# Layer 0, step one: four engines in source order, in-place tiles in one deep ring, normalizing in place, Toeplitz rows on the storing queue

## The chip, the cores and the metric

The kernel runs on one core of a Trainium2 chip. The core has five engines with a queue each: TensorE (PE, with its weight loads shown apart as PEld), VectorE (DVE), ScalarE (ACT), GpSimd (POOL) and SyncE (SP, which here only issues transfers). Transfers (DMAs) are issued by SP, ACT or POOL and carried out by 16 DMA engines. The metric is the time of one execution on the device in microseconds (us); lower is better.

## What is computed

Four layers, each adding a block's output to x (8 images of 56 x 56 positions and 192 channels, float32). The change concerns the first part of layer 0 alone:

```python
def _gn(v, G=32, eps=1e-5):              # group norm over 6 channels x all positions
    g = v.reshape(B_, H_, W_, G, C_ // G)
    ...
    return ((g - m) / jnp.sqrt(s + eps)).reshape(v.shape)

# layer 0, D1 = 576
    p = jax.nn.silu(x @ p_w.T + p_b)
    q = jax.nn.silu(x @ q_w.T + q_b)
    v = jax.nn.silu(x @ v_w.T + v_b)
    ...
    a1 = _rpe_mlp(rpe_input, t1_w0, ...) * decay      # 111 coefficients a channel
    a2 = _rpe_mlp(rpe_input, t2_w0, ...) * decay
    qv = q * v
    o1 = _toeplitz(qv.reshape(b * h, w, D1), a1).reshape(b, h, w, D1)   # along a row
    o2 = _toeplitz(jnp.transpose(qv, (0, 2, 1, 3)).reshape(b * w, h, D1), a2)   # along a column
    ...
    out = p * (o1 + o2)
    return out @ o_w.T + o_b
```

## The kernel before

**Two steps through DRAM.** Layer 0 runs as two steps. Step one computes qv for all eight images and writes it to two DRAM arrays, `left` (rows as they are) and `right` (transposed in the image), in blocks of 64 channels ("subs", nine of them). Behind the qv rows each array holds 64 Toeplitz rows a sub, made from the coefficients. Step two (`layer0_mix`) loads blocks of both (`layer0_block`, tiles `lt` and `rt` of 1.8 MB each), multiplies them on TensorE, gates with p and projects. The change is in step one; later stages are as they were.

**Step one.** Per image b: `layer0_load` (L353) fetches x, a tile of 128 x 3 x 1568 (two halves of the image times 64 channels, three channel blocks), from POOL's queue. `layer0_in` (L358) takes twelve pieces of statistics (L157), two tiny matmuls over the groups (L176) with a square root on ACT between (L186), and writes the normalized image to another tile `xn` (L371, DVE). `layer0_qv` (L374) then runs over 14 pairs of image rows (`PH`) and two halves n of the 576 outputs. One such (i, n) is called a group below; there are 8 x 14 x 2 = 224. A group is 12 matmuls (q and v, three channel blocks, both image halves s), recorded as 24 because each float32 matmul is two records; then, for each s, the bias out of PSUM (L393, DVE), SiLU in place (L394, ACT) and q*v (L395, DVE) into the tile `qv`. After the second n, three stores for each s go out from SP's queue: one to `left` (L398) and two to `right` (L403). The `qv` ring has 3 tiles, `act` 4, and PSUM holds 4 tiles of two banks under the tag "qv", shared with every small matmul of this step.

**What is put between.** `between[i]` lists small jobs that are traced after row pair i: the coefficient network (`toeplitz_rows`, L227, 13 pieces with PSUM tiles of their own), Toeplitz rows and zero rows (L295 and L300, 128 DRAM to DRAM transfers issued by ACT), the attention mask of layer 1 (`build_bias_mask`), its weights (`layer1_weights`), and `layer0_in` of the next image after row pair 4.

**What sets the order.** In step one no order is written out: the build's scheduler ranks the traced instructions by its own estimate of times and lays down each engine's queue. Each engine then works through its queue strictly in that order and waits where an operand isn't there. Later stages have stretches under `tc.manual_schedule`, in which the named engines keep the order of the source.

Of the kernel before, what the change touches and what calls it, by code (L numbers as in the profile page):

```python
# [10 lines left out]
F32 = mybir.dt.float32  # L11
AF = mybir.ActivationFunctionType
ALU = mybir.AluOpType
# [4 lines left out]
B, H, W, C = 8, 56, 56, 192  # L18
NT = H * W
HC = 96  # L20
TT = 392
NTT = NT // TT
D1 = 576
DCH = [(0, 128), (128, 128), (256, 128), (384, 128), (512, 64)]
NSUB = D1 // 64
# [37 lines left out]
NH = NT // 2  # L63
NTH = NH // TT
PH = NPAIR // 2
# [24 lines left out]
def kernel(ctx: ExitStack, tc: tile.TileContext, a: dict, out: bass.AP):  # L90
    nc = tc.nc
# [21 lines left out]
    gmath = resident("gmath")  # L113
# [7 lines left out]
    eps5 = const.tile([128, 1], F32, name="eps5")  # L121
# [14 lines left out]
    none = dram.tile([QR], F32, name="none")  # L136
# [17 lines left out]
    def gn_piece(st, x, t):  # L154

        for j in range(3):
            nc.vector.bn_stats(st[:, j, t], x[:, j, bass.ts(t, TT)])  # L157

    def gn_aggregate(st, mv):
        nc.vector.bn_aggr(mv, st.rearrange("p j t s -> p (j t s)"))  # L160

    def gn_finish(mv, sc, sh, pool, psum, ptag):


        n = mv.shape[1]

        def over_groups(v, name):
            if ptag == "mm":
                ps = psum.tile([128, 512], F32, name=name, tag="mm", bufs=3)
            elif ptag == "y":  # L170
                ps = psum.tile([128, TT], F32, name=name, tag="y")
            elif ptag == "gn":
                ps = psum.tile([128, 3], F32, name=name, tag="gn", bufs=1)
            else:
                ps = psum.tile([128, 2, 512], F32, name=name, tag=ptag)[:, 0]
            nc.tensor.matmul(ps[:, 0:n], gmath, v, start=True, stop=True)  # L176
            return ps[:, 0:n]

        mean = pool.tile([128, n], F32, name="gh_mean")
        nc.vector.tensor_copy(mean, over_groups(mv[:, :, 0], "gh_m"))  # L180
        d = pool.tile([128, n], F32, name="gh_d")
        nc.vector.tensor_tensor(d, mv[:, :, 0], mean, ALU.subtract)
        nc.vector.tensor_tensor(d, d, d, ALU.mult)
        nc.vector.tensor_tensor(d, d, mv[:, :, 1], ALU.add)
        yield
        nc.scalar.activation(sc, over_groups(d, "gh_v"), AF.Sqrt, bias=eps5)  # L186
        nc.vector.reciprocal(sc, sc)
        nc.vector.scalar_tensor_tensor(sh, mean, -1.0, sc, ALU.mult, ALU.mult)

    def run(steps):  # L190
        for _ in steps:
            pass
# [34 lines left out]
    def toeplitz_rows(psum, pool, rows):  # L227
# [16 lines left out]
        k = 1  # L244
        while k < 55:
            n = min(k, 55 - k)
# [9 lines left out]
        for i in range(2):  # L256
            m = f"m{i + 1}_"
            h = pool.tile([32, 111], F32, name=f"h{i}")
# [3 lines left out]
        for l in range(3):  # L262
            yield
            for i in range(2):
                ps = psum.tile([128, 2, 512], F32, name="hps", tag="qv")
# [6 lines left out]
        for c, (d0, M) in enumerate(DCH):  # L272
            yield
            cos = []
            for i in range(2):
                ps = psum.tile([128, 2, 512], F32, name="aps", tag="qv")
# [7 lines left out]
            for i in range(2):  # L284
                ps = psum.tile([128, 2, 512], F32, name="cps0", tag="qv")
# [7 lines left out]
        parts = [z[toep_row(0):].rearrange("(s k) n -> k s n", k=64) for z in (left, right)]  # L293

        def row(i, w0):  # L295
            nc.scalar.dma_start(
                parts[i][w0], coef[i][:, 55 - w0:111 - w0].rearrange("s l d -> s (l d)")
            )

        def zeros(i, k):  # L300
            nc.scalar.dma_start(parts[i][k], none.partition_broadcast(NSUB))

        rows += [lambda i=i, k=k: zeros(i, k) for i in range(2) for k in range(W, 64)]
        rows += [lambda i=i, w0=w0: row(i, w0) for i in range(2) for w0 in range(W)]
# [48 lines left out]
    def layer0_load(b, pool):  # L353
        x = pool.tile([128, 3, NH], F32, name="x0")
        nc.gpsimd.dma_start(x, a["x"][b])
        return x

    def layer0_in(b, x, pool, psum):  # L358

        sc, sh = scsh[:, 0, b:b + 1], scsh[:, 1, b:b + 1]  # L360
        st = pool.tile([128, 3, NTH, 6], F32, name="gh_st")
        for t in range(NTH):
            gn_piece(st, x, t)
        mv = pool.tile([128, 1, 2], F32, name="gh_mv")
        gn_aggregate(st, mv[:, 0])
        run(gn_finish(mv, sc, sh, pool, psum, "qv"))
        xn = pool.tile([128, 3, NH], F32, name="xn0")
        n = NH if b else TT
        for t in range(NH // n):
            ts = bass.ts(t, n)  # L370
            nc.vector.tensor_scalar(xn[:, :, ts], x[:, :, ts], sc, sh, ALU.mult, ALU.add)  # L371
        return xn

    def layer0_qv(b, xn, pool, psum, w_qv, b_qv, between):  # L374

        lv, rv = (
            z[qv_row(b, 0):qv_row(b, 0) + NSUB * W].rearrange("(s h) (w d) -> s h w d", h=W, d=64) for z in (left, right)
        )
        for i in range(PH):
            qv = pool.tile([2 * W, 2, D1], F32, name="qv", bufs=3)  # L380
            for n in range(2):
                ns = slice(n * D1 // 2, (n + 1) * D1 // 2)
                ps = [psum.tile([2 * W, 2, 512], F32, name=f"qv{s}", tag="qv") for s in range(2)]
                for which in range(2):
                    for j in range(3):
                        for s in range(2):
                            nc.tensor.matmul(  # L387
                                ps[s][:, which, 0:D1 // 2], xn[64 * s:64 * s + 64, j, bass.ts(i, 2 * W)],
                                w_qv[64 * s:64 * s + 64, j, which, ns], start=(j == 0), stop=(j == 2),
                            )  # L390
                for s in range(2):
                    act = pool.tile([2 * W, 2, D1 // 2], F32, name="act", bufs=4)
                    nc.vector.tensor_tensor(act, ps[s][:, :, 0:D1 // 2], b_qv[:, :, ns], ALU.add)  # L393
                    nc.scalar.activation(act, act, AF.Silu)  # L394
                    nc.vector.tensor_tensor(qv[:, s, ns], act[:, 0], act[:, 1], ALU.mult)  # L395
            for s in range(2):
                h0 = H // 2 * s + 2 * i
                nc.sync.dma_start(  # L398
                    lv[:, h0:h0 + 2].rearrange("s h w d -> (h w) s d"),
                    qv[:, s].rearrange("t (s d) -> t s d", d=64),  # L400
                )
                for r in range(2):
                    nc.sync.dma_start(  # L403
                        rv[:, :, h0 + r].rearrange("s w d -> w s d"),
                        qv[r * W:(r + 1) * W, s].rearrange("w (s d) -> w s d", d=64),
                    )
            for step in between[i]:
                step()

    def layer0_block(b, s, raws):  # L410

# [910 lines left out]
    with ExitStack() as st:  # L1322
        pool = st.enter_context(tc.tile_pool(reuse_waits="tile", name="qv", bufs=2))
        psum = st.enter_context(tc.tile_pool(reuse_waits="tile", name="qvp", bufs=4, space=PSUM))
        w_qv = resident("w_qv", nc.scalar, pool)
        b_qv = pool.tile([2 * W, 2, D1], F32, name="b_qv", bufs=1)
        nc.scalar.dma_start(b_qv.rearrange("p a d -> p (a d)"), a["b_qv"].partition_broadcast(2 * W))
        tz = st.enter_context(tc.tile_pool(reuse_waits="tile", name="tz", bufs=2))
        x = layer0_load(0, pool)
        xn = layer0_in(0, x, pool, psum)  # L1330
        rows, masks = [], []
        coefs, bias = toeplitz_rows(psum, tz, rows), build_bias_mask(psum, tz, masks)
        centred = layer1_weights(tz, psum)

        def pop(todo, n=1):
            for _ in range(min(n, len(todo))):
                todo.pop(0)()

        for b in range(nimg):

            between = {i: [lambda i=i: pop(rows, 2 if i % 3 == 1 else 1)] for i in range(PH)}
            if b == 0:
                for i in range(PH):
                    between[i].insert(0, lambda: [next(coefs, None) for _ in range(2)])
                between[10].append(lambda: next(bias, None))
            elif b == 1:
                between[6].append(lambda: next(bias, None))
                between[12].append(lambda: pop(masks))
            elif b == 2:
                for i in range(6):  # L1350
                    between[2 * i].append(lambda: next(centred, None))
            if b:
                between[9].append(lambda: pop(masks))
            ahead = []
            if b + 1 < nimg:
                x = layer0_load(b + 1, pool)
                between[4].append(lambda: ahead.append(layer0_in(b + 1, x, pool, psum)))
            layer0_qv(b, xn, pool, psum, w_qv, b_qv, between)
            xn = ahead[0] if ahead else None
        pop(rows, len(rows))  # L1360
        pop(masks, len(masks))
    with ExitStack() as st:
# [8 lines left out]
        images, x = ExitStack(), []  # L1371
# [312 lines left out]
```

## Time and profile before

| | us |
|---|---|
| median of three runs | 5757.5 |
| lowest, highest | 5750.73, 5760.37 |
| the profiled run | 5770.6 |
| its span | 5768.8 |
| PE, DVE, ACT, POOL busy in the span | 5181.2, 3336.5, 2169.1, 1420.2 |
| first and last matmul record of step one (L387) | 28.6 and 846.7 |
| last store of step one issued until | 857.7 |

The profile is one execution. A group of instructions is given as line, engine, operation, names, shapes, count, busy time, mean duration in ns, and the idle time of the engine before it with what ended that. PEclk or "granted clock" is the share of TensorE's full clock that it was allowed. A line "A <- B" among the waits says that A stood for B. The DMA share is the mean busy share of the 16 engines. The granted clock over the whole span is 0.957.

### The profile page before, as it was taken

What the parts mean: (1) busy time and instruction counts of PE and PEld (TensorE: products, weight loads), DVE (VectorE), ACT (ScalarE), POOL (GpSimd) and SP (SyncE); (2) the same over time, 40 slices, a digit from 0 to 9 for tenths busy, and PEclk for the clock granted to TensorE, in tenths of its full rate; (3) what the DMA queues carried; (4) which work ended last, traced back from release to release, by engine and by line L of the source; (5) the groups of instructions that cost most, each with busy time, mean ns of one, the idle gap of its engine ahead of it and who ended that gap; (6) DMA issues with size and microseconds to landing.
All of it is one profiled execution on the core that took longest, in us unless ns stands there. A gap on an engine that the chain in (4) does not pass through costs nothing. (4 is left out here: it accounts for less than half of the span.)

```text
span 5768.8 us, 116138 instructions
## 1 busy us (share of the span) xinstructions
PE 5181.2 (90%) x50342; PEld 3376.1 (59%) x50342; DVE 3336.5 (58%) x4710; ACT 2169.1 (38%) x2908; POOL 1420.2 (25%) x1107
## 2 busy tenths in 40 slices
PE   6898998999899979999997989999788798999999
PEld 4568765666666645555554657676344597444444
DVE  5777774555555546566665868888778202433331
ACT  2333443333333423333332004555476400433333
POOL 2100004444444424433342013333101101100100
PEclk8999999999999989999998989999899899999999
DMA  6888986776677633222222866666687598212211
GB/s 179 204 211 216 206 182 258 264 264 258 247 262 264 222 92 82 69 75 76 69 65 76 260 235 218 227 232 209 160 232 215 222 328 295 78 62 77 76 41 26
DMA packets 721922, 1013.94 MB, mean 176 GB/s; under 512 B 486376, under 2 KB 645444, under 8 KB 694644
## 3 DMA queue, kind: packets, MB, share of 16 engines
q1 hardware_dynamic: 706352, 940.12, 52.4%
q0 software_dynamic: 8512, 40.62, 2.1%
q10 hardware_dynamic: 6548, 25.78, 1.4%
q8 instruction: 396, 6.49, 0.5%
q14 instruction: 114, 0.93, 0.0%
HBM read 676.92 MB, written 345.97 MB: 177 GB/s over the span
## 5 line engine op out<-in xcount | busy, mean ns | idle before, releaser
L387 PE MATMUL qv<-w_qv_sb,xn 64*112 64x288 f32 x5376 | 711.3, 421 | 48.6 <-DVE act L393 45.4
L425 POOL COPY lc<-lt 128x896 f32<-128x896 f32 (+1 forms) x320 | 552.5, 1751 | 640.9 <-PE op L433 543.1
L387 PEld LDWEIGHTS qv<-w_qv_sb,xn 64*112 64x112 f32 x5376 | 558.5, 182 | 195.5 <-DVE act L393 58.1
L394 ACT ACTIVATE act<-act 112x576 f32<-112x576 f32 x448 | 300.6, 683 | 466.8 <-DVE act L393 427.4
L433 PE MATMUL op<-rc,lc 128*56 128x56 f32 x9216 | 339.1, 221 | 102.1 <-POOL lc L425 64.9
L433 PEld LDWEIGHTS op<-rc,lc 128*56 128x56 f32 x9216 | 307.8, 135 | 177.9 <-POOL lc L425 103.5
L1289 PE MATMUL ph<-y,w_sb 64*128 64x392 f32 x2304 | 397.7, 497 | 6.5 <-ACT hid L1293 6.5
L1300 PE MATMUL po<-hid,w_sb 128*64 128x392 f32 x2304 | 386.3, 494 | 0.0
L393 DVE TENSOR_TENSOR act<-qv,b_qv 112x576 f32<-112x576 f32 x448 | 320.7, 752 | 92.7 <-PE qv L387 92.4
L1307 DVE TENSOR_TENSOR x<-x,z 128x392 f32<-128x392 f32 x96 | 67.0, 698 | 524.2 <-ACT z L1305 524.2
L425 ACT COPY rc<-rt 128x896 f32<-128x896 f32 (+1 forms) x160 | 256.3, 1606 | 249.7 <-PE op L433 227.2
L805 PE MATMUL qk_ps<-xr,wg 64*96 64x392 f32 x1536 | 334.2, 538 | 1.8 <-DVE xr L752 1.7
L1016 PE MATMUL cv<-zc,wt 128*128 128x224 f32 x1536 | 313.6, 356 | 24.2 <-DMA zc<-pd 24.2
L1016 PEld LDWEIGHTS cv<-zc,wt 128*128 128x128 f32 x1536 | 291.0, 190 | 67.5 <-issue 51.2
L1289 PEld LDWEIGHTS ph<-y,w_sb 64*128 64x128 f32 x2304 | 220.0, 188 | 175.9 <-issue 25.5
L445 PE MATMUL pj<-xn,w_p_sb 64*128 64x392 f32 x1536 | 309.8, 511 | 12.4 <-DVE xn L533 8.2
L1190 PE MATMUL cps<-zc,wt 128*128 128x224 f32 x1536 | 300.2, 356 | 18.2 <-DMA zc<-zd 16.8
L1190 PEld LDWEIGHTS cps<-zc,wt 128*128 128x128 f32 x1536 | 289.6, 189 | 28.7 <-issue 21.3
L466 PE MATMUL y<-pp,w_o_sb 128*64 128x392 f32 x1536 | 285.9, 501 | 4.8 <-DVE x L474 4.1
L459 DVE TENSOR_TENSOR pp<-pp,ot 128x784 f32<-128x784 f32 x128 | 124.2, 970 | 284.8 <-ACT pp L450 272.9
L1300 PEld LDWEIGHTS po<-hid,w_sb 128*64 128x64 f32 x2304 | 162.7, 137 | 213.8 <-issue 213.8
L1031 POOL TENSOR_TENSOR rows<-rows,loc 128x896 f32<-128x896 f32 x96 | 220.8, 2300 | 261.7 <-ACT rows L1027 201.9
(233 smaller groups left out, 8895.1 us busy)
## 6 DMA issues: line engine op xcount, KB each, us to landing
lt<-left SPq DMA_DIRECT2D x72, 1792.0 KB
rt<-right SPq DMA_DIRECT2D x72, 1792.0 KB
left<-qv SPq DMA_DIRECT2D x224, 252.0 KB
right<-qv SPq DMA_DIRECT2D x448, 126.0 KB
wt<-in_band_dram SPq DMA_DIRECT2D x23, 2048.0 KB
wt<-in_band_dram SPq DMA_DIRECT2D x11, 4096.0 KB
zc<-pd SPq DMA_DIRECT2D x187, 232.0 KB
pd<-pt SPq DMA_DIRECT2D x7, 5568.0 KB
```

The source lines that it names most:

```text
L387: nc.tensor.matmul(ps[s][:, which, 0:D1 // 2], xn[64 * s:64 * s + 64, j, bass.ts(i, 2 * W)], w_qv[64 * s:64 * s + 64, j, which, ns], start ...
L393: nc.vector.tensor_tensor(act, ps[s][:, :, 0:D1 // 2], b_qv[:, :, ns], ALU.add)
L394: nc.scalar.activation(act, act, AF.Silu)
L425: copy(c[:, 0:nu], raw.rearrange("p (w u d) -> p u d w", u=nu, d=64 // nu)[:, :, d0:d0 + 8])
L433: nc.tensor.matmul(op[64 * u:64 * u + W, i, :], lc[:, u, i], rc[:, u, i], start=True, stop=True)
L445: nc.tensor.matmul(ps[0:M, s, 0:TT], w_p[64 * s:64 * s + 64, j, d0:d0 + M], xn[64 * s:64 * s + 64, j, ts], start=(j == 0), stop=(j == 2),)
L466: nc.tensor.matmul(y[64 * s:64 * s + 64], w_o[0:M, c, 64 * j:64 * j + 64], pp[0:M, s], start=(c == gated[0][0]), stop=(c == gated[-1][0]),)
L805: nc.tensor.matmul(in_pairs(ps[s]), wg[64 * s:64 * s + 64, j, c0:c0 + HC], in_slots(xr[64 * s:64 * s + 64], (3 * g + j) * GW), start=(j == ...
L1016: nc.tensor.matmul(dst, wt[:, c4 + i, 128 * q:128 * q + 128], zc[:, :, c4 + i, q:q + NPAIR], start=(q == 0), stop=(q == 1),)
L1190: nc.tensor.matmul(dst.rearrange("p (b n) -> p b n", n=NPAIR), wt[:, c4 + i, q * OP:(q + 1) * OP], zc[:, :, c4 + i, q:q + NPAIR], start=(q ...
L1289: nc.tensor.matmul(ps[:, s, 0:TT], w0[64 * s:64 * s + 64, j, m * 128:(m + 1) * 128], y[64 * s:64 * s + 64, j, ts], start=(j == 0), stop=(j ...
L1300: nc.tensor.matmul(ps[64 * s:64 * s + 64], w1[:, m, 64 * j:64 * j + 64], hid[:, m, s], start=(m == 0), stop=(m == 5),)
```

## The change

Five things change in step one.

1. PE, ACT, DVE and POOL keep the order of the source (`manual_schedule`); SP's queue is still laid down by the scheduler. `layer0_in` becomes a generator that is advanced by one piece after each group from the eighth on.
2. A group's outputs are 5 subs or 4 subs (320 or 256 columns) in turn, not 288 each. Bias, SiLU and the product all work in one tile `act`, of which there are 14; there is no `qv` tile. A group's product is traced one group later, for s = 0 on DVE and for s = 1 on POOL, followed by its stores: three per s and group, where there were three per s and pair of groups.
3. x is normalized in place in four pieces, on DVE for the first image and on POOL for the others. So a tile of x is in use until its image's last matmul, and the load of the image after next waits for that.
4. Toeplitz and zero rows are issued by SP, three of them in every four groups, and cannot begin before the coefficients are done.
5. `between` counts groups, not row pairs. The first coefficient piece and the 42 small loads of the mask's table (`raw`) are traced ahead of the first image.

```diff
@@ -293,12 +293,12 @@
...
         def row(i, w0):
-            nc.scalar.dma_start(
+            nc.sync.dma_start(
                 parts[i][w0], coef[i][:, 55 - w0:111 - w0].rearrange("s l d -> s (l d)")
             )
 
         def zeros(i, k):
-            nc.scalar.dma_start(parts[i][k], none.partition_broadcast(NSUB))
+            nc.sync.dma_start(parts[i][k], none.partition_broadcast(NSUB))
@@ -360,52 +360,77 @@
         sc, sh = scsh[:, 0, b:b + 1], scsh[:, 1, b:b + 1]
         st = pool.tile([128, 3, NTH, 6], F32, name="gh_st")
         for t in range(NTH):
-            gn_piece(st, x, t)
-        mv = pool.tile([128, 1, 2], F32, name="gh_mv")
-        gn_aggregate(st, mv[:, 0])
-        run(gn_finish(mv, sc, sh, pool, psum, "qv"))
-        xn = pool.tile([128, 3, NH], F32, name="xn0")
-        n = NH if b else TT
-        for t in range(NH // n):
-            ts = bass.ts(t, n)
-            nc.vector.tensor_scalar(xn[:, :, ts], x[:, :, ts], sc, sh, ALU.mult, ALU.add)
-        return xn
-
-    def layer0_qv(b, xn, pool, psum, w_qv, b_qv, between):
+            for j in range(3):
+                nc.vector.bn_stats(st[:, j, t], x[:, j, bass.ts(t, TT)])
+                yield
+        mv = pool.tile([128, 2], F32, name="gh_mv")
+        gn_aggregate(st, mv)
+        yield
+        yield
+        of = [psum.tile([128, 2, 512], F32, name=n, tag="qv")[:, 0, 0:1] for n in ("gh_m", )]
+        nc.tensor.matmul(of[0], gmath, mv[:, 0:1], start=True, stop=True)
+        mean, d = (pool.tile([128, 1], F32, name=n) for n in ("gh_mean", "gh_d"))
+        nc.vector.tensor_copy(mean, of[0])
+        nc.vector.tensor_tensor(d, mv[:, 0:1], mean, ALU.subtract)
+        nc.vector.tensor_tensor(d, d, d, ALU.mult)
+        nc.vector.tensor_tensor(d, d, mv[:, 1:2], ALU.add)
+        yield
+        yield
+        of.append(psum.tile([128, 2, 512], F32, name="gh_v", tag="qv")[:, 0, 0:1])
+        nc.tensor.matmul(of[1], gmath, d, start=True, stop=True)
+        nc.scalar.activation(sc, of[1], AF.Sqrt, bias=eps5)
+        yield
+        nc.vector.reciprocal(sc, sc)
+        nc.vector.scalar_tensor_tensor(sh, mean, -1.0, sc, ALU.mult, ALU.mult)
+        for t in range(NTH):
+            xs = x[:, :, bass.ts(t, TT)]
+            (nc.gpsimd if b else nc.vector).tensor_scalar(xs, xs, sc, sh, ALU.mult, ALU.add)
+            if t < 2:
+                yield
+
+    def layer0_qv(b, x, pool, psum, w_qv, b_qv, between):
 
         lv, rv = (
             z[qv_row(b, 0):qv_row(b, 0) + NSUB * W].rearrange("(s h) (w d) -> s h w d", h=W, d=64) for z in (left, right)
         )
+        later = []
+
+        def multiply(i, s0, s1, acts):
+            n = 64 * (s1 - s0)
+            for s in range(2):
+                eng = (nc.vector, nc.gpsimd)[s]
+                eng.tensor_tensor(acts[s][:, 0, 0:n], acts[s][:, 0, 0:n], acts[s][:, 1, 0:n], ALU.mult)
+            for s in range(2):
+                h0 = H // 2 * s + 2 * i
+                qv = acts[s][:, 0, 0:n].rearrange("t (s d) -> t s d", d=64)
+                nc.sync.dma_start(lv[s0:s1, h0:h0 + 2].rearrange("s h w d -> (h w) s d"), qv)
+                for r in range(2):
+                    nc.sync.dma_start(rv[s0:s1, :, h0 + r].rearrange("s w d -> w s d"), qv[r * W:(r + 1) * W])
+
         for i in range(PH):
-            qv = pool.tile([2 * W, 2, D1], F32, name="qv", bufs=3)
-            for n in range(2):
-                ns = slice(n * D1 // 2, (n + 1) * D1 // 2)
+            for at, (s0, s1) in enumerate(((0, 5), (5, NSUB))):
+                n = 64 * (s1 - s0)
                 ps = [psum.tile([2 * W, 2, 512], F32, name=f"qv{s}", tag="qv") for s in range(2)]
                 for which in range(2):
                     for j in range(3):
                         for s in range(2):
                             nc.tensor.matmul(
-                                ps[s][:, which, 0:D1 // 2], xn[64 * s:64 * s + 64, j, bass.ts(i, 2 * W)],
-                                w_qv[64 * s:64 * s + 64, j, which, ns], start=(j == 0), stop=(j == 2),
+                                ps[s][:, which, 0:n], x[64 * s:64 * s + 64, j, bass.ts(i, 2 * W)],
+                                w_qv[64 * s:64 * s + 64, j, which, 64 * s0:64 * s1], start=(j == 0), stop=(j == 2),
                             )
+                acts = [pool.tile([2 * W, 2, 320], F32, name="act", bufs=14) for _ in range(2)]
                 for s in range(2):
-                    act = pool.tile([2 * W, 2, D1 // 2], F32, name="act", bufs=4)
-                    nc.vector.tensor_tensor(act, ps[s][:, :, 0:D1 // 2], b_qv[:, :, ns], ALU.add)
-                    nc.scalar.activation(act, act, AF.Silu)
-                    nc.vector.tensor_tensor(qv[:, s, ns], act[:, 0], act[:, 1], ALU.mult)
-            for s in range(2):
-                h0 = H // 2 * s + 2 * i
-                nc.sync.dma_start(
-                    lv[:, h0:h0 + 2].rearrange("s h w d -> (h w) s d"),
-                    qv[:, s].rearrange("t (s d) -> t s d", d=64),
-                )
-                for r in range(2):
-                    nc.sync.dma_start(
-                        rv[:, :, h0 + r].rearrange("s w d -> w s d"),
-                        qv[r * W:(r + 1) * W, s].rearrange("w (s d) -> w s d", d=64),
+                    nc.vector.tensor_tensor(
+                        acts[s][:, :, 0:n], ps[s][:, :, 0:n], b_qv[:, :, 64 * s0:64 * s1], ALU.add
                     )
-            for step in between[i]:
-                step()
+                for s in range(2):
+                    nc.scalar.activation(acts[s][:, :, 0:n], acts[s][:, :, 0:n], AF.Silu)
+                for step in later:
+                    step()
+                later = [lambda now=(i, s0, s1, acts): multiply(*now)]
+                for step in between[2 * i + at]:
+                    step()
+        later[0]()
@@ -1327,10 +1352,15 @@
         nc.scalar.dma_start(b_qv.rearrange("p a d -> p (a d)"), a["b_qv"].partition_broadcast(2 * W))
         tz = st.enter_context(tc.tile_pool(reuse_waits="tile", name="tz", bufs=2))
         x = layer0_load(0, pool)
-        xn = layer0_in(0, x, pool, psum)
         rows, masks = [], []
         coefs, bias = toeplitz_rows(psum, tz, rows), build_bias_mask(psum, tz, masks)
         centred = layer1_weights(tz, psum)
+        st.enter_context(tc.manual_schedule(
+            engines={mybir.EngineType.PE, mybir.EngineType.Activation, mybir.EngineType.DVE, mybir.EngineType.Pool}
+        ))
+        next(coefs)
+        next(bias)
+        run(layer0_in(0, x, pool, psum))
 
         def pop(todo, n=1):
             for _ in range(min(n, len(todo))):
@@ -1338,25 +1368,27 @@
 
         for b in range(nimg):
 
-            between = {i: [lambda i=i: pop(rows, 2 if i % 3 == 1 else 1)] for i in range(PH)}
+            between = {i: [lambda i=i: pop(rows, 1 if i % 4 else 0)] for i in range(2 * PH)}
             if b == 0:
-                for i in range(PH):
-                    between[i].insert(0, lambda: [next(coefs, None) for _ in range(2)])
-                between[10].append(lambda: next(bias, None))
+                for i in range(2 * PH):
+                    between[i].append(lambda: next(coefs, None))
             elif b == 1:
-                between[6].append(lambda: next(bias, None))
-                between[12].append(lambda: pop(masks))
+                between[13].append(lambda: next(bias, None))
+                between[25].append(lambda: pop(masks))
             elif b == 2:
                 for i in range(6):
-                    between[2 * i].append(lambda: next(centred, None))
+                    between[4 * i + 1].append(lambda: next(centred, None))
             if b:
-                between[9].append(lambda: pop(masks))
-            ahead = []
+                between[19].append(lambda: pop(masks))
+            ahead = iter(())
             if b + 1 < nimg:
-                x = layer0_load(b + 1, pool)
-                between[4].append(lambda: ahead.append(layer0_in(b + 1, x, pool, psum)))
-            layer0_qv(b, xn, pool, psum, w_qv, b_qv, between)
-            xn = ahead[0] if ahead else None
+                following = layer0_load(b + 1, pool)
+                ahead = layer0_in(b + 1, following, pool, psum)
+                for i in range(7, 2 * PH):
+                    between[i].append(lambda: next(ahead, None))
+            layer0_qv(b, x, pool, psum, w_qv, b_qv, between)
+            run(ahead)
+            x = following
         pop(rows, len(rows))
         pop(masks, len(masks))
     with ExitStack() as st:
```

In the instruction order as built, SP has 800 DMAs more (672 stores, 128 rows), ACT 128 fewer, POOL 252 instructions more and DVE 231 fewer. No block of step two is issued before the last store of step one. From the second block of step two on, each engine has nearly the order that it had.

## The prediction

> **What bounds the stage now.** The change touches only layer 0's first step, the program's first 858 us. The chain that ended last does not help: its pieces begin at 4033 us. So I read stretches, then waits, then the timeline. The page's groups first:
>
> ```profile
> L387 PE MATMUL qv<-w_qv_sb,xn 64*112 64x288 f32 x5376 | 711.3, 421 | 48.6 <-DVE act L393 45.4
> ...
> L394 ACT ACTIVATE act<-act 112x576 f32<-112x576 f32 x448 | 300.6, 683 | 466.8 <-DVE act L393 427.4
> ...
> L393 DVE TENSOR_TENSOR act<-qv,b_qv 112x576 f32<-112x576 f32 x448 | 320.7, 752 | 92.7 <-PE qv L387 92.4
> ```
>
> A group is 24 of the L387 matmul records (half the outputs of two row pairs); there are 5376/24 = 224. DVE needs 2 x 752 for the bias and 2 x 461 ns for q*v (L395), 2.43 us a group; ACT 2 x 683 = 1.37 us. Stretches of 25 us for L387 alone (busy and count of PE, of weight loads, granted clock, DMA share, GB/s):
>
> ```profile
> 50.00:75.00 25.00, 13.59 (x88) 9.39 (x90) 0.73 0.86 239
> ...
> 275.00:300.00 25.00, 25.00 (x210) 18.56 (x208) 1.00 0.95 214
> ...
> 325.00:350.00 25.00, 14.29 (x90) 10.13 (x88) 0.73 0.73 199
> ...
> 775.00:800.00 25.00, 25.00 (x210) 18.56 (x208) 1.00 0.88 181
> ```
>
> At its best TensorE does 210 records in 25 us: 2.86 us a group. 224 of them are 641 us, but the groups take from 28.6 to 847 us, 3.65 us each. Some 175 us are lost in holes, with the clock down to 0.73 beside them. The waits over the first 1120 us (total, times, longest), then one hole in the timeline:
>
> ```profile
> ACT act L394 <- DVE act L393: 427.4, 230, 12.3
> ...
> DVE gh_st L157 <- DMA x<-in_x_dram: 40.3, 6, 7.7
> ```
>
> ```profile
> 324.75 0.54 POOL L355 DMA_DIRECT2D x<-in_x_dram  x1 [53.37 <-DVE xn L371]
> ...
> 336.31 1.97 DVE L157 BATCH_NORM_STATS2 gh_st<-x 128x6 f32<-128x392 f32 x4 [6.74 <-DMA x<-in_x_dram]
> ...
> 339.03 0.68 ACT L394 ACTIVATE act<-act 112x576 f32<-112x576 f32 x1 [8.68 <-DVE act L393]
> ...
> 344.80 14.20 PE L387 MATMUL qv<-w_qv_sb,xn 64*112 64x288 f32 x94 [2.23 <-DVE act L393]
> ```
>
> The reader sees an ordering fault. The next image's load starts at 324.75, DVE's queue already has that image's statistics at its head, and DVE stands 6.74 us for the transfer; finished matmuls keep their PSUM tiles, so TensorE stops too. Image 0 loses most: between 29 and 150 us only 552 records (23 groups, 5.3 us each).
>
> The other resource is the stores. Their queue, at PE's full pace without Toeplitz rows and with them:
>
> ```profile
> 785.13 0.31 SPq L398 DMA_DIRECT2D left<-qv  x1
> 785.49 1.57 SPq L403 DMA_DIRECT2D right<-qv  x2
> ```
>
> ```profile
> 159.37 0.90 SPq L398 DMA_DIRECT2D left<-qv  x1
> 160.31 1.93 SPq L403 DMA_DIRECT2D right<-qv  x2
> ```
>
> Each group issues such a triple. It costs 1.9 to 2.4 us without rows in flight, 2.7 to 2.9 with them, and then SP hardly rests. All engines by stretches (PE, PEld, DVE, ACT, POOL, clock, DMA share, GB/s):
>
> ```profile
> 725.00:850.00 125.00, 122.07 (x1008) 90.26 (x1004) 101.08 (x172) 58.63 (x87) 2.60 (x3) 1.00 0.88 181
> 850.00:900.00 50.00, 27.23 (x506) 19.77 (x508) 18.16 (x20) 18.06 (x17) 25.32 (x16) 0.76 0.89 342
> ```
>
> **Two rules of the skill.** "DMA: Bandwidth & Descriptors", Specifications, asks for transfers of at least 512 B for line rate. The two rows above agree: with 256 B pieces (64 floats) a share of 0.88 moves 181 GB/s, with long rows 0.89 moves 342. Splitting a store by subs leaves the pieces at 256 B, so I keep the DMA work per byte. The same page, "Issuing engines are not separate DMA queues", says that all queues use the same 16 engines and another issuer saves only issue time. The trace agrees: rows on ACT's queue raise SP's triple from about 2.2 to 2.75 us. So I book the rows' DMA time as unchanged, and only their issue as moved.
>
> **Part by part.**
> *Source order, with statistics spread one per group from the eighth group on.* It removes the holes. The load of image b+1 is issued as image b starts (its tile is free when b-1's last matmul is done); 7 groups are 20 us, the load's median landing 11.5 us, so DVE should find it there. Seven image turns and image 0's preparation held the 175 us. Not all goes: each of image 0's 13 coefficient steps takes two of the four PSUM tiles and makes TensorE wait for two biases, about 0.75 + 0.75 us less a matmul of its own, 1.2 us; 16 us in all. The two statistics matmuls shift the ring by one tile, about 2 us an image; the Sqrt table loads stay (2 x 1.28 us, under ACT's slack of 1.5 us a group). At the front POOL must issue 42 `raw` loads at 617 ns (26 us) before the second image and its first product, at about 41 us. By then four groups are done; the ring of 14 tiles holds 7 groups, so this is hidden. Without that cover it would cost some 10 us.
> *Product.* One of two goes to POOL. It has no such row here; the nearest are
>
> ```profile
> L1214 POOL TENSOR_TENSOR yl<-yl,dwb 128x448 f32<-128x448 f32 x12 | 11.2, 936 | 54.8 <-DMA yl<-yd 54.8
> ...
> L1135 POOL TENSOR_SCALAR zp<-x2o,sc,sh 128x1568 f32<-128x1568 f32 x24 | 43.8, 1836 | 263.0 <-DVE sh L188 150.0 <-PE tp L1097 56.8 <-PE po L1110 26.8
> ```
>
> 2.1 ns an element (2.6 in L1031): 0.6 to 0.75 us for 288 on average, of a 2.9 us group. Normalizing is 4 x 1176 elements at 1.17 ns, 5.5 us an image, in the last four groups; the first piece serves the next four slices, so TensorE need not wait for the last. POOL thus holds 28 x 0.7 + 5.5 = 25 of 81 us. DVE falls to 2 x 0.752 + 0.461 = 1.96 us a group and loses a 2.73 us block an image. Neither is the bound; worth nothing alone.
> *Chunks of 5 and 4 subs.* The same columns and weight loads: 3.2 and 2.6 us in turn, zero on average.
> *Stores.* Twice as many, half as long: 6 per group. SP has to issue 1344 instead of 672, and 128 rows that ACT issued at 0.69 us (88 us, leaving ACT). Smallest issues in the trace are 0.31 (left) and 0.42 us (right): 2 x 0.31 + 4 x 0.42 = 2.3 us a group, the floor if it is per instruction; in proportion to descriptors it stays 2.2. Rows add 0.75 x 0.69 = 0.5 us a group while they last. Ceiling: if today's means (0.65 and 1.03 us) did not shrink at all, 5.4 us. I take 2.3 to 2.6, plus rows.
> *DMA work.* 0.88 x 2.90 = 2.55 us a group of full share. The mean share from 29 to 850 us is 0.85: 698 us. Of that 571 are stores, 7 x 6.3 = 44 images (2.35 MB at the 384 GB/s that 342/0.89 gives), 19 the four blocks of step two fetched early, which leaves 64, under 0.45 us a row.
>
> **The sum.** Start 28.6 us. Image 0: 28 x 2.95 + 16 = 99, to 128. Images 1 to 5 carry 21 rows each: 71.4 + 6.3 + 9.4 = 87 us of DMA against 80 us of TensorE; at a share of 0.97, 90 each, to 578. Image 6 (11 rows) 85, to 663. Image 7 81 and small waits 4, to 748; last stores about 753 instead of 857.7. So 105 us come off the step, now at the pace of stores, no longer of an order.
> Then something is given back. In the built order of the changed kernel no block of step two is fetched before the last store; before, two left and two right blocks were there (issues from 400.8 us on). Four blocks of 1.8 MB are 7.3/0.384 = 19 us, less the 4 us that the kernel before waited from its last issue to its next load: 15 us (5 if the first gate's wait for x, 11.4 us there, covers some; 20 if nothing does). Later stages have the same order. Net 90 to 95 us: the profiled 5770.6 (span 5768.8) becomes 5678. The median of the runs shown is 0.23% under the profiled run, so 5665.
>
> **Rivals.**
> (a) PE's pace: packets' time stretches when there is slack, so the share isn't work that must be done. For it: 210 records in 25 us with rows in flight at 0.95. Against: SP at 23 to 25 of 25 us there. 28.6 + 99 + 7 x 84 = 716, gain 141 - 15 = 126: 5632. 25%.
> (b) SP's issue at 3.4 us a group (half sizes cost a little over the floor, rows on top): 28.6 + 224 x 3.4 + 15 = 805, gain 53 - 15 = 38: 5720. 12%.
> (c) Slower: one mechanism, at SP's queue: an issue has a price that doesn't fall with size, or the eight completion semaphores that the DMAs of the hardware queues use in turn hold SP back (eight half-size stores in flight; a 14 KB transfer alone took 1.97 us until its reader's issue). It decides from (857.7 - 15 - 28.6 - 10)/224 = 3.59 us a group, 0.53 us a DMA with rows. At 0.6 us: 6 x 0.6 + 0.4 = 4.0 us, 933 us, +75 + 15: 5848. For it: right stores cost 1.03 us in the mean and SP is full; against: that follows contention (4.4 us a triple beside an image load, 2.1 alone). 11%.
> (d) Nothing gained: new in-order waits (POOL, ACT, SP) eat what the holes gave. 2%.
>
> **Numbers.** The forecast has 50%. Range 5625 to 5735: it takes in (a) and (b) and leaves out (c) and little else. Under 0.2% (11 us) a measurement can't tell from no change. Faster 0.50 + 0.25 + 0.12 less a little = 0.86; same 0.03; slower 0.11.
>
> **What would show it.** Right: no DVE wait for x over 2 us, groups under 3.3 us from image 1 on, the L387 successor's last record between 730 and 755, DMA share above 0.93 in the row phase, a hole of 10 to 20 us of little TensorE work at the turn to step two. Wrong: SP issues over 0.5 us each with PE's clock falling, or waits of multiply and bias for DMAs.

## The result, and the profile after

| | before | after |
|---|---|---|
| median of the runs beside each other (4 of each), us | 5757.2 | 5851.4 |
| ratio, 95% interval | | 1.0163, 1.0145 to 1.0180 |
| span of the profiled run, us | 5768.8 | 5843.2 |
| last matmul record of step one, us | 846.7 | 903.8 |
| last store of step one issued until, us | 857.7 | 928.7 |
| first product of step two, us | 854.4 | 941.3 |

The change makes the kernel slower by 94 us. The forecast was 5665, and its range ended at 5735. Step two starts 86.9 us later, so the loss is in step one and at the turn to step two.

The groups of the page after, against those of L387, L393 and L394 before (line, engine, operation, shapes, count, busy and mean ns, idle time before and what ended most of it):

```profile
L417 PE MATMUL qv<-w_qv_sb,x 64*112 64x256 f32 (+1 forms) x5376 | 761.8, 422 | 95.0 <-DVE act L423 88.9
...
L423 DVE TENSOR_TENSOR act<-qv,b_qv 112x640 f32<-112x640 f32 x448 | 331.8, 755 | 352.5 <-DMA right<-act 239.6
L427 ACT ACTIVATE act<-act 112x640 f32<-112x640 f32 x448 | 300.0, 683 | 547.3 <-DVE act L423 417.0
...
L402 POOL TENSOR_TENSOR act<-act 112x320 f32<-112x320 f32 x224 | 178.6, 797 | 581.7 <-ACT act L427 506.2
```

No engine works longer on an instruction than before (bias 755 for 752 ns, SiLU 683 for 683). What is new stands behind the bar: the bias now waits 239.6 us for `right<-act`, a store that still holds the ring tile it wants. Before, it waited for the matmul. The waits over the first 1000 us (total, times, longest):

```profile
DVE act L423 <- DMA right<-act: 239.6, 193, 9.1
...
ACT act L427 <- DMA right<-act: 97.8, 33, 8.4
...
DVE rc L450 <- DMA rt<-right: 43.1, 4, 31.4
```

The old wait of the statistics for x, 40.3 us before, is gone. Next, stretches of 25 us of L417 alone (PE and weight loads with counts, granted clock, DMA share, GB/s):

```profile
400.00:425.00 25.00, 23.30 (x167) 17.18 (x168) 1.00 0.79 169
825.00:850.00 25.00, 25.00 (x211) 21.52 (x209) 1.00 0.77 161
```

With rows in flight TensorE does 167 records, 3.6 us a group. Without rows (825 us) it does its full 211, though the last image as a whole, which has no rows beside it, still takes 87.8 us, 3.1 a group. In both stretches the DMA share is under 0.8, where the same stage reaches 0.96 in e12 below, so the DMA engines are not what is short. SP's queue shows what is. Its timeline near 400 us (start, duration, operation, count):

```profile
401.61 0.36 SPq L406 DMA_DIRECT2D left<-act  x1
402.01 0.99 SPq L408 DMA_DIRECT2D right<-act  x2
403.10 0.38 SPq L406 DMA_DIRECT2D left<-act  x1
403.52 1.00 SPq L408 DMA_DIRECT2D right<-act  x2
404.57 0.73 SPq L296 DMA_DIRECT2D left<-coef  x1
405.40 0.40 SPq L406 DMA_DIRECT2D left<-act  x1
```

SP issues without a pause: a triple takes 1.5 us from start to start although it is half the size, and a row puts 0.83 us between two triples. In this stretch SP waits for nothing, neither a product nor a completion. Added up over 150 to 895 us, per group: 3.1 us for six store issues, 0.33 for the gaps between instructions, 0.5 for the row share, 3.9 us together. The largest of SP's waits between 150 and 850 us, before and then after:

```profile
SPq L398 <- DVE qv L395: 134.0, 81, 12.5
```

```profile
SPq L406 <- DVE act L423: 9.5, 23, 1.2
```

Before, SP had time to spare and stood for products. After, all its waits in these 700 us come to some 20 us.

At the end of the step the ring lets TensorE run ahead, so 25 us of stores are left when the last matmul is done. Only then does the first block load of step two leave (timeline, the idle time before in brackets):

```profile
927.70 0.95 SPq L408 DMA_DIRECT2D right<-act  x2
928.69 0.61 SPq L442 DMA_DIRECT2D lt<-left  x1
929.35 0.59 SPq L442 DMA_DIRECT2D rt<-right  x1
...
941.26 3.24 PE L458 MATMUL op<-rc,lc 128*56 128x56 f32 x64 [37.05 <-DVE rc L450]
```

TensorE stands 37 us here. Before, it stood 7.3 us:

```profile
854.38 1.90 PE L433 MATMUL op<-rc,lc 128*56 128x56 f32 x35 [7.31 <-DVE rc L425]
```

The 86.9 us are thus 57.1 (last matmul), 13.9 (stores left behind it: 24.9 us for 11.0) and 15.9 (from the last store to the first product: +12.6 us for -3.3, where the blocks had been there early).

### The profile page after: what moved, and what is told of

The parts are those of the page before. It is cut to its first block, busy times and chain, and to the rows that moved or that the text cites. A ratio compares the mean times of both kernels' runs of the same rounds, so it can differ in the third digit from the quotient of the medians.

```text
span 5843.2 us, 118073 instructions
## 1 busy us (share of the span) xinstructions
PE 5222.5 (89%) x50342; PEld 3392.1 (58%) x50342; DVE 3255.9 (56%) x4479; ACT 2167.4 (37%) x2908; POOL 1628.3 (28%) x1359
## 5 line engine op out<-in xcount | busy, mean ns | idle before, releaser
L417 PE MATMUL qv<-w_qv_sb,x 64*112 64x256 f32 (+1 forms) x5376 | 761.8, 422 | 95.0 <-DVE act L423 88.9
L417 PEld LDWEIGHTS qv<-w_qv_sb,x 64*112 64x112 f32 x5376 | 576.3, 180 | 270.3 <-DVE act L423 151.8
L423 DVE TENSOR_TENSOR act<-qv,b_qv 112x640 f32<-112x640 f32 x448 | 331.8, 755 | 352.5 <-DMA right<-act 239.6
L427 ACT ACTIVATE act<-act 112x640 f32<-112x640 f32 x448 | 300.0, 683 | 547.3 <-DVE act L423 417.0
L402 POOL TENSOR_TENSOR act<-act 112x320 f32<-112x320 f32 x224 | 178.6, 797 | 581.7 <-ACT act L427 506.2
L875 POOL TENSOR_TENSOR e<-e,mx 128x1176 f32<-128x1176 f32 x64 | 140.0, 2187 | 561.4 <-DVE mx L874 550.8
```

What stands on the lines that cost most here:

```text
L417: nc.tensor.matmul(ps[s][:, which, 0:n], x[64 * s:64 * s + 64, j, bass.ts(i, 2 * W)], w_qv[64 * s:64 * s + 64, j, which, 64 * s0:64 * s1], ...
L423: nc.vector.tensor_tensor(acts[s][:, :, 0:n], ps[s][:, :, 0:n], b_qv[:, :, 64 * s0:64 * s1], ALU.add)
L427: nc.scalar.activation(acts[s][:, :, 0:n], acts[s][:, :, 0:n], AF.Silu)
```

## The experiments

Theories at first: **A**, each issue on SP has a price that hardly falls with size; **B**, so many transfers in flight set the pace, whoever issues them; **C**, the order of the source and its waits cost the time. Later **D**, a limit that all transfers share, and **K**, rows confined to few DMA engines. Times are medians, with ratios to the kernel before run beside them and their 95% intervals; e5, e10 and e15 were run once each.

**e1: rows back on ACT.**

```diff
-            nc.sync.dma_start(
+            nc.scalar.dma_start(
                 parts[i][w0], ...
```

> The changed kernel with its Toeplitz and zero rows issued by ACT again, as before the change. Theory A (each DMA has a price of issue on its queue: 0.49 us for a half-size store with its gap, 0.83 us for a row, and SP's sum sets the pace): 128 x 0.83 = 106 us leave SP, which is then at 2.95 us a group, about PE's own pace; 5745 to 5775 us. Theory B (the number of transfers in flight sets the pace, whoever issues them): no gain, over 5830. Theory C (the source order's in-order waits cost the time, SP is only full because stores wait): no gain or worse, over 5830.

5856.3 us, 1.0172 (1.0152 to 1.0193). No gain; A missed. ACT then stood behind SP's stores (150 to 850 us; in the changed kernel this wait is 90.3 us):

```profile
ACT act L427 <- DMA right<-act: 297.7, 67, 14.5
```

In the built kernel SP's and ACT's transfers take turns on the same eight completion semaphores (the trace has these eight for both), so a row on ACT can wait for SP's backlog. This run alone decided nothing.

**e2: whole stores again** (products of both chunks into one tile `qvt` of 9 subs, 8 of them, 6 `act`; three stores for each s once both chunks are there).

```diff
-                eng.tensor_tensor(acts[s][:, 0, 0:n], acts[s][:, 0, 0:n], acts[s][:, 1, 0:n], ALU.mult)
-            for s in range(2):
+                eng.tensor_tensor(qvs[s][:, 64 * s0:64 * s1], acts[s][:, 0, 0:n], acts[s][:, 1, 0:n], ALU.mult)
+            for s in range(2 if s1 == NSUB else 0):
```

> The changed kernel with the two chunks' products put into one tile of 576 columns and three whole stores per s and pair of groups, as before the change; rows stay on SP. Theory A: a pair's six stores cost 4.4 to 5.5 us as in the kernel before, plus 1.5 rows at 0.83: 2.85 to 3.4 us a group against 3.5 now, so 5700 to 5800. Theory B: twice the bytes in flight, a gain as well, 5700 to 5780. Theory C: no gain, over 5830.

5725.1 us, 0.9945 (0.9931 to 0.9960): 126 us less than the changed kernel. The last matmul is at 792.6. A and B had both said this; C falls.

**e3: e2 with the rows on ACT.**

> Whole stores and rows on ACT together. Theory A: SP has 2.2 to 2.75 us a group, so PE or the DMA engines set the pace at 2.9 to 3.1 us and the last store is out at 720 to 760 us: 5660 to 5700. Theory B: as with whole stores alone, within 20 us of that run. Theory C: over 5800.

5710.7 us, 0.9915 (0.9887 to 0.9943). With the rows off SP's queue two blocks of each side are fetched early again: TensorE's gap at the turn is 5.9 us, where e2 has 30.4. A's range is missed by 11 us and B's fits, so whole stores alone do not part the two; e5 does.

**e9: the changed kernel without the written order.**

```diff
-        st.enter_context(tc.manual_schedule(
-            engines={mybir.EngineType.PE, mybir.EngineType.Activation, mybir.EngineType.DVE, mybir.EngineType.Pool}
-        ))
```

> The changed kernel without the source order: the scheduler lays down all queues in step one, all else (half-size stores, rows on SP, ring, POOL's product) as changed. Theory A: SP's issues are the same, so within 30 us of the changed kernel's 5851, or slower by the holes of the old order. Theory C: back to about 5757.

5864.8 us, 1.0187 (1.0161 to 1.0213). C falls again: the order isn't what costs.

**e6: the kernel before with its stores alone split.**

```diff
             for s in range(2):
                 h0 = H // 2 * s + 2 * i
+                for s0, s1 in ((0, 5), (5, NSUB)):
...
-                    lv[:, h0:h0 + 2].rearrange("s h w d -> (h w) s d"),
+                        lv[s0:s1, h0:h0 + 2].rearrange("s h w d -> (h w) s d"),
```

> The kernel before, with its stores alone cut as the change cuts them (5 and 4 subs): 1344 stores for 672, order, product, rows and normalizing as they were. A: SP needs 2.94 us a group without rows and more with ACT's rows beside them, some of it inside the old holes: 5780 to 5850, most of the change's loss without the change's gain. B and D: within 15 us of 5757.

5859.9 us, 1.0174 (1.0157 to 1.0191): 103 us more than before, and 10 above A's range. The split alone brings the whole loss; B and D, which said no change, fall.

**e5: each store of the changed kernel cut in two again.**

```diff
+                for a0, a1 in ((s0, s0 + 2), (s0 + 2, s1)):
+                    qv = acts[s][:, 0, 64 * (a0 - s0):64 * (a1 - s0)].rearrange("t (s d) -> t s d", d=64)
...
```

> The changed kernel with each half-size store cut in two again (2 and 3 or 2 and 2 subs): 12 stores a group, the same bytes in the same 256-byte pieces. A: 12 x 0.42 to 0.49 + 0.6 for rows = 5.6 to 6.5 us a group, 6300 to 6500 us. B (so many transfers in flight, each shorter when smaller) at most +0.3 us a group, below 5950. D (work of the DMA engines, the same bytes and pieces): 5840 to 5870.

6397.4 us: 546 more for 1344 stores more and not a byte more, 0.41 us each. A holds and B and D fall again. The two kernels can be compared with nothing beside the stores, after the last matmul. First the changed kernel's SP timeline, and its stretch from 916 to 928 us (PE, PEld, DVE, ACT, POOL, clock, DMA share, GB/s):

```profile
921.33 0.36 SPq L406 DMA_DIRECT2D left<-act  x1
921.74 0.95 SPq L408 DMA_DIRECT2D right<-act  x2
922.78 0.37 SPq L406 DMA_DIRECT2D left<-act  x1
923.19 0.98 SPq L408 DMA_DIRECT2D right<-act  x2
924.27 0.37 SPq L406 DMA_DIRECT2D left<-act  x1
```

```profile
916.00:928.00 12.00, 0.00 (x0) 0.00 (x0) 0.00 (x0) 0.00 (x0) 0.00 (x0) 0.50 0.89 188
```

Then e5's timeline and stretch:

```profile
1443.30 0.38 SPq L407 DMA_DIRECT2D left<-act  x1
1443.72 0.91 SPq L409 DMA_DIRECT2D right<-act  x2
1444.73 0.34 SPq L407 DMA_DIRECT2D left<-act  x1
1445.11 0.88 SPq L409 DMA_DIRECT2D right<-act  x2
1446.03 0.38 SPq L407 DMA_DIRECT2D left<-act  x1
```

```profile
1440.00:1465.00 25.00, 0.00 (x0) 0.00 (x0) 0.00 (x0) 0.00 (x0) 0.00 (x0) 0.50 0.50 115
```

Triples of 4 and 5 subs start 1.45 to 1.52 us apart, those of 2 and 3 subs 1.28 to 1.43. Half the bytes save a tenth, and the DMA share falls from 0.89 to 0.50. As a line through the means (1.49 and 1.34 us), a triple costs 1.19 us whatever its size, 0.40 us a store. That is an estimate from two points, and at the larger one the DMA engines are nearly full themselves; e5's total, which doesn't rest on it, says 0.41. Why an issue has this price the runs don't show.

**e7: the left stores on POOL.**

```diff
-                nc.sync.dma_start(lv[s0:s1, h0:h0 + 2].rearrange("s h w d -> (h w) s d"), qv)
+                nc.gpsimd.dma_start(lv[s0:s1, h0:h0 + 2].rearrange("s h w d -> (h w) s d"), qv)
```

> The changed kernel with the left stores (448 of the 1344) issued by POOL, rows staying on SP. A: SP has 4 x 0.56 + 0.75 x 0.8 = 2.8 us a group, below TensorE's pace, so 5700 to 5750, if POOL, busy some 30 of 81 us an image, finds time for 2 issues a group at 0.5 to 1 us. D: 5835 or more.

5741.7 us, 0.9971 (0.9953 to 0.9988), 110 less than the changed kernel with as many transfers of the same size. The same stores cost POOL 0.77 us each, so this only moves the price to another queue.

**e4: the rows on POOL** (as e1, with `nc.gpsimd`).

> The changed kernel with the Toeplitz and zero rows issued by POOL, whose transfers run in a queue of their own kind with completions of their own, so that neither ACT nor SP stands behind them. A (SP's price per issue, 0.49 us a half-size store, sets the pace): SP has 6 x 0.49 = 2.94 us a group left of 3.5 to 3.7, the first step ends some 100 to 140 us earlier, 5715 to 5755 us. D (a limit that all transfers share, whoever issues them, as e1 seemed to show): no gain, 5835 to 5860.

5838.9 us, 1.0143 (1.0128 to 1.0158). A missed again, without ACT's waits to blame. SP's timeline with POOL's row:

```profile
400.94 0.55 POOL L296 DMA_DIRECT2D left<-coef  x1
401.10 0.97 SPq L408 DMA_DIRECT2D right<-act  x2
402.17 0.35 SPq L406 DMA_DIRECT2D left<-act  x1
402.56 1.80 SPq L408 DMA_DIRECT2D right<-act  x2
404.46 0.35 SPq L406 DMA_DIRECT2D left<-act  x1
404.85 0.98 SPq L408 DMA_DIRECT2D right<-act  x2
```

Behind this row one pair of store issues takes 1.80 us where 0.98 is the rule. Counted from the trace for all 112 coefficient rows, the store issues of the next 4 us exceed their quiet lengths (0.37 us left, 0.46 right) by 0.88 us in the median. So the row, 126 KB in nine pieces of 14 KB, takes from SP's stores what it no longer takes from SP's queue.

**e10: the rows traced last.**

```diff
-            between = {i: [lambda i=i: pop(rows, 1 if i % 4 else 0)] for i in range(2 * PH)}
+            between = {i: [] for i in range(2 * PH)}
```

> The changed kernel with its Toeplitz and zero rows traced behind the last image: SP's queue as built has 23 of the 128 among the stores and 105 in one burst behind the last store. A (an issue price, rows on top): 2.95 us a group without a row, so the last matmul of the step near 29 + 16 + 224 x 2.95 + 23 x 0.8 = 725 us instead of 904, the last row issued near 725 + 15 + 105 x 0.8 = 825 instead of the last store at 928, and 5740 to 5775 us in all. If rows cost the stores nothing (the half-size stores alone make the 3.55 us a group): last matmul at 850 or later and 5880 or more.

5846.1 us. The last matmul came at 825.6, not 725, and the last store at 850.5, 78 us before that of the changed kernel: 78/105 = 0.74 us a row. The forecast was 100 us too early. At 1.5 us a triple the stores would need 672 of the 808 us from first to last. The rest is image 0, where SP was busy for only 58 of its first 82 us, and single long issues beside image loads and mask transfers: left stores took 0.76 us in the mean from 525 to 550 us, beside an image load, and 0.38 from 575 to 600. So with hardly a row among them the stores still need 3.5 us a group (images 1 to 5 take 99.3 us each). The burst then took all of the gain, so the total didn't move, and neither range held.

**e15: e4 with each of its 112 coefficient rows written twice.**

> e4 (rows issued by POOL) with each of the 112 coefficient rows written twice, the second time over the first. If a row's own transfer holds the stores up by some 0.8 us whoever issues it, as e4's longer store issues behind a row suggest: 112 x 0.8 = 90 us more than e4's 5838.9, 5900 to 5945. If e4 failed to gain for another reason (POOL's waits, the blocks fetched early): 5835 to 5860.

6010.4 us, more than either theory said. POOL waited for the first copy before it issued the second (150 to 850 us):

```profile
POOL left L297 <- DMA left<-coef: 135.5, 42, 8.9
...
POOL right L297 <- DMA right<-coef: 93.1, 32, 5.8
```

These 229 us hold up the products as well, so this run doesn't tell what a row costs.

**e16, e18, e17: rows in shorter pieces.** e4, the changed kernel and e12 (below) with each coefficient row cut in 16 x 9 pieces of 896 bytes:

```diff
-                parts[i][w0], coef[i][:, 55 - w0:111 - w0].rearrange("s l d -> s (l d)")
+                parts[i][w0].rearrange("s (e n) -> e s n", e=16),
+                coef[i][:, 55 - w0:111 - w0].rearrange("s l d -> s (l d)").rearrange("s (e n) -> e s n", e=16),
```

> e4 (half-size stores, rows issued by POOL) with each coefficient row written as 16 x 9 pieces of 896 bytes for 9 pieces of 14 KB. K (a row confined to nine of the sixteen DMA engines holds the stores up there; the Trainium skill, DMA: Bandwidth & Descriptors, how many engines a transfer uses): 112 rows x some 0.4 us less, 5780 to 5815. Bytes (126 KB a row cost the stores the same however they are cut) or a price per transfer: 5825 to 5855.

5772.5 us (20 runs), 1.0024 (1.0016 to 1.0033): 66 us less than e4, 0.59 us a row. Its timeline beside a row:

```profile
409.02 0.58 POOL L296 DMA_DIRECT2D left<-coef  x1
409.98 0.36 SPq L407 DMA_DIRECT2D left<-act  x1
410.39 1.11 SPq L409 DMA_DIRECT2D right<-act  x2
411.60 0.37 SPq L407 DMA_DIRECT2D left<-act  x1
412.01 0.99 SPq L409 DMA_DIRECT2D right<-act  x2
```

The pair behind this row takes 1.11 us. It isn't so behind each one (one of three between 398 and 415 us still costs 2.32), but the excess behind a row falls from 0.88 to 0.23 us in the median, and the mean store issue (150 to 750 us) falls too: right 0.59 for 0.65, left 0.45 for 0.52. The gain is more than K forecast.

> The changed kernel, rows on SP, in 16 x 9 pieces. SP's issue is the price here (0.73 us a row, seen as SP's own time): 5840 to 5865, no gain. K deciding here too: 5795 to 5825.

5844.9 us, 1.0149 (1.0129 to 1.0169). On SP's own queue cutting the row doesn't help: the total is 7 us less than the changed kernel's. The row's own issue gets shorter (0.53 us for 0.73), which is 22 us over 112 rows, but left stores get longer (0.49 for 0.43 in the mean, 150 to 750 us). The forecast of no gain held; its row price of 0.73 did not.

> e12 (whole stores, rows issued by POOL) with the rows in 16 x 9 pieces. K: nine engines were the busiest, 112 x 0.3 us less than e12's 5705.8, 5665 to 5690. Bytes: 5695 to 5720; if 896-byte pieces cost more engine time than 14 KB ones, up to 5730.

5714.2 us, 0.9918 (0.9898 to 0.9939): with whole stores nothing comes of it.

**e19: e16 with eight parts for sixteen** (`e=8`, pieces of 1792 bytes).

> e16 with the rows in 8 x 9 pieces of 1792 bytes, the eight outermost. If the number of DMA engines decides (K): at most eight carry a row, no better than e4's nine: 5825 to 5860. If the length of a piece decides (short pieces let stores in between): near e16's 5772.5, 5765 to 5790.

5777.0 us, 1.0040 (1.0025 to 1.0054), e16's time. The section "Why a DMA increments its semaphore by 16 and not by 1" of the Trainium skill's "DMA: Bandwidth & Descriptors" says how many DMA engines a transfer uses, by the sizes of the slowest dimensions of its two sides. By that rule eight carry a row here and nine in e4, and yet e19 gains 62 us, so K falls if the rule holds here; the section names an exception for transfers that POOL issues, and no view tells the engine of a packet. What does differ is the length of a packet, as the traces record them (150 to 700 us):

| | packets a row | bytes | mean us of one | engine time a row, us |
|---|---|---|---|---|
| e4 | 9 | 14336 | 0.90 | 8.1 |
| e16 | 32 | 4480 and 3584 | 0.36 and 0.15 | 8.0 |
| e19 | 24 | 5376 | 0.34 | 8.3 |

The DMA engines' work on a row is the same in all three, and so is the number of transfers; the longest packet isn't. The length of the pieces is thus the reading that fits all three: long ones hold SP's stores up. That an issue waits until such a packet is through would fit too, but no view shows it.

**e12: whole stores, rows on POOL.**

> The changed kernel with whole stores and the rows issued by POOL. DMA work bounds it, as e3 (whole stores, rows on ACT, 5710.7): 5695 to 5720; blocks of step two are fetched early again, which the rows on SP kept out. Faster than e3 by up to 10 if ACT's standing behind the shared completions cost e3 anything.

5705.8 us, 0.9912 (0.9888 to 0.9936), the fastest median, though e3 and e17 lie within its interval. Its stretches (engines in the order PE, PEld, DVE, ACT, POOL, then clock, DMA share, GB/s) and its matmul group:

```profile
300.00:325.00 25.00, 25.00 (x200) 21.73 (x198) 20.24 (x36) 11.90 (x18) 15.05 (x22) 1.00 0.98 239
...
150.00:775.00 625.00, 604.02 (x4764) 526.22 (x4762) 448.19 (x759) 276.23 (x406) 268.49 (x375) 0.98 0.96 228
```

```profile
L418 PE MATMUL qv<-w_qv_sb,x 64*112 64x256 f32 (+1 forms) x5376 | 700.5, 411 | 32.8 <-DVE act L424 20.7
```

A DMA share of 0.96 over 625 us: now the DMA engines are close to their limit, and TensorE's idle time before its matmuls is 32.8 us for 95.0. All else in the change, with whole stores and the rows on POOL, is thus worth some 50 us; only the split made it a loss.

## Why the prediction was wrong

**The step that failed** is *Stores*: "I take 2.3 to 2.6, plus rows". That is about what a group's one whole triple cost before (1.9 to 2.4 us), so it let twice as many issues cost the same. The two models under it were 0.31 and 0.42 us an issue, and a cost in proportion to descriptors. Neither holds. The 0.31 and 0.42 were the smallest issues in the trace, not usual ones, and left out the gap after each instruction. Half-size stores take 0.37 and 0.49 us at their quietest, with gaps 1.49 us a triple, so 3.0 us a group. The mean over the step was 3.4: most issues keep their quiet length, but between 150 and 850 us 50 of them took 0.9 us or more, 86 us together. With its rows SP needed 3.9 us a group. The forecast had SP at 3.1 at most and let DMA work set the pace, 3.2 us (90 us an image). So the last matmul came at 903.8 us and not at 748, the last store at 928.7 and not at 753: 176 of the 186 us by which 5665 missed.

What it came to is rival (c), to which 11% was given and which said 5848. Its pace of 4.0 us a group was 3.9, its point of decision, 0.53 us a DMA, was passed (3.9 us over 6.6 transfers is 0.59). Of its two mechanisms the price of an issue is shown (e5, e6, e7). Against the completion semaphores stands that between 150 and 850 us SP waited 0.5 us in all for a transfer, and that for 45 of the 50 long issues the semaphore waited for was there before the issue began. Its 0.6 us a DMA was an assumption and not read from a line, so that 5848 came within 4 us of the measured 5851 is in part luck. The rival was given too small a chance because "that follows contention" was read from stores of full size, where a DMA share of 0.88 to 0.95 can hide the floor.

**Rows.** "0.75 x 0.69 = 0.5 us a group" was the right size on SP (0.73 an issue, 0.5 a group), but its cause was half understood. The text kept the rows' DMA time as unchanged "and only their issue as moved". e4 shows that a row off SP still costs the stores nearly the same (12 us of the loss come back), and e16 and e19 that it is so only with 14 KB pieces.

**The turn.** 15 us were booked for blocks that aren't fetched early: 15.9 measured. Not booked were 13.9 us of stores that the deep ring leaves behind the last matmul (the sum allowed 5 us between the two). That "no block of step two is fetched before the last store" holds in the runs with the rows and all stores on SP. e1, e3, e4 and e12, with the rows elsewhere, fetch blocks early, and so does e7 (from 734 us on), with the left stores on POOL.

**What held.** *Source order*: the statistics wait no more for x, and with whole stores (e12) images 1 to 5 take 91.8 us each, forecast 90; image 1 begins at 144, forecast 128. *DMA work*: e12 runs at a share of 0.96, forecast 0.97. *Product*: 0.80 us on POOL, forecast 0.6 to 0.75, on no path that counts. *Chunks*: no row of the page shows a cost. But e12's last store comes at 802, forecast 753: image 0 and the stores left behind the last matmul make most of that, so even without the split 5665 was too low by some 40 us.

The Trainium skill's section "Issuing engines are not separate DMA queues" says that a further issuing engine saves only the time it takes to issue, usually small beside the transfer. Here it was not small: SP's queue was full while the DMA engines were busy 0.79 of the time, and 448 stores moved to POOL were worth 110 us (e7). The prediction cited this section for the rows and didn't ask what it says of the issues themselves.

## What to carry to other kernels

Before a transfer is split, count transfers, not bytes: take the start-to-start distance of back-to-back issues on the queue, and compare the number of issues times that with the time the compute needs. A floor read from large transfers may be hidden by the DMA engines, so look for the shortest ones in a quiet stretch and include the gap. And where a queue is full, moving one kind of transfer to another issuer can be worth little if its long pieces still hold up the rest (e4: 12 us).

## What the hardware showed that was not expected

- A store issued by SP has a part of some 0.4 us that doesn't fall with size: a triple takes 1.49 us at 4.5 subs in the mean and 1.34 at 2.25 (0.40 as a line through both), and 1344 stores more without a byte more cost 546 us.
- An issue can lengthen while other queues' transfers run, though hardly a semaphore is waited for (0.7 us for transfers between 150 and 850 us in e4): two right stores took 0.98 us, and 1.80 behind a row from POOL.
- Rows from POOL in nine pieces of 14 KB cost SP's stores 0.6 us a row more than the same bytes in pieces of 896 or 1792 bytes (5838.9 us for 5772.5 and 5777.0).
- The same left store costs 0.42 us on SP and 0.77 us on POOL.
